# A rarely taken way moved behind the usual one: flag, checks, gathers and row steps in another order

## The chip, the core and the metric

The kernel runs on one core of a Trainium2 chip. A core has a matrix engine (PE), a vector engine (DVE), a scalar engine (ScalarE, ACT in the profile), GpSimd (POOL), SyncE (SP), which here only issues transfers, and 16 DMA engines. Each engine works through its own list of instructions in order; semaphores make one wait for another. The metric is the device time of the whole kernel in microseconds (us).

## The reference

Input are `x` (2708 nodes x 128 features) and a sparse non-negative matrix `adj` (2708 x 2708). Four graph layers follow each other, each `x = layernorm(x + layer(x, adj))`:

```python
# 0: normalised adjacency
h = (d[:, None] * (adj + I) * d[None, :]) @ x;  h @ W.T + b
# 1: attention
XW = x @ W;  s_col = XW @ a[:f];  s_row = XW @ a[f:]
den = exp(leaky_relu(s_row[:, None] + s_col[None, :], 0.01))
num = adj @ den
att = where(num != 0, den / num, 0)
H = adj @ (att @ XW)
# 2: hyperbolic layer: matvec, bias, logmap, adj @ xt, expmap, relu
# 3: (adj > 0) @ x and (adj < 0) @ x times node weights, adj @ x times edge weights, biases by the diagonals
```

Only the piece from the end of layer 0 to layer 1, and the very end, are touched here.

## The kernel before

**Two ways.** Layer 1 as written needs a product of 2708 x 2708 matrices. The kernel avoids it. `den[i, j]` is an exponential of a sum, on either side of a kink, so it splits into a product of a factor for i and one for j on each side. If the nodes are sorted by their scores in 26 groups (`GM`) of at most 126, then for one group most of the numerator is a sum over whole rows of `adj`, carried from group to group, and only the group's own 126 rows need gathering. This holds only if the scores and row sums are in bounds, no element of `adj` is negative and the nodes fit the groups. `good`, `okb`, `below0` and the product `gps` check that and leave `flag_i` (L1313 to L1324): 0 where the fast way may be taken. If it is not, the general way (`dense_attention`, `general_rest`) computes everything after layer 0 densely. With the inputs of the reference the fast way is taken. The flag is read into a register of each engine (L1833); a branch leads to the general way, which stands first, or past it to the fast one.

**Before the flag.** Layer 0 streams `adj` in blocks of 4 x 128 rows by 512 columns. Its end normalises `x`, projects it (`xw`, the scores `rc`; L989 to L1008), stores `xw` to DRAM as `xw_d` (L1009) and counts for each node how many sampled scores lie above it (L1048). Meanwhile SyncE fetches most blocks of `adj` again as `B` (`fill_tile`, L821), for the *row steps*: `whole_sum` (L800), called through `sum_rows`, multiplies the 128 rows of one tile by `e1` and adds them to one row of sums, `tot`. There are 22 steps, nine products each; they are strewn over the sort stage so that PE has work while other engines sort. A block's place is freed when its four steps are done, and the next block fetched into it. At the end ScalarE copies `tot` into `carry0` (L1390), the start of the carried sum.

**Sorting.** DVE finds the borders of the groups: `prev` from the counts (L1206), transposed (L1220), then 26 dependent comparisons with an accumulator, `v` (L1237). Between the row steps PE spreads scores over partitions (`rb`) for `q_b` (L1228). From the borders come one-hot matrices `oh` for the rows' order (i = 0) and the columns' (i = 1), and the packed values `val` (tile number, partition, score in three bf16 `terms`, occupancy; L1278 to L1330). Products with a triangle of ones, `low` (L1293, L1303), count places, giving `slot`; for each of 22 tiles a one-hot `ohs` (L1345) and a product into `list` (L1347) scatter the nodes into 26 x 128 lists. List 0 gives `row_i`, which rows of `adj` to gather; list 1 gives `xw_i`, `gj_l`, `occ_l`, `inval`. `group_matrix` (L707, L708) makes from them the weight matrix of a group; the first three go into `w_first`.

**Groups.** `grouped_attention` takes the columns in two halves of 1354. For each half and group: gather 128 rows by an indirect transfer from POOL (L1427, four buffers), copy the two carried rows into the next group's gather (L1475), multiply (`num`, L1471), take the reciprocal as `exp(-ln)` on ScalarE (L1476, L1483), `att = max(q_b * gj, 1)` (L1465, three buffers) times that (L1484), and aggregate with the group's gathered rows of `xw` into `uacc` (L1436). The rows of `xw` (L1405) are gathered in the first half, one group's after its gather of `adj`. `fast_rest` then does the end of layer 1 and layers 2 and 3 in products with `adj`, streamed in pieces `cb`.

**Order.** A scheduler places the instructions of each engine; `queued(engine)` fixes the order of the marked ones, and `tc.issue_after(x)` places one behind x. Tiles come from pools; memory of a closed pool is used again by a later one, and a tile on it waits for the last users.

## Time and profile before

| | us |
|---|---|
| median of 3 runs | 922.99 (921.04 to 926.29) |
| the profiled execution itself | 920.86 |
| its span, first to last instruction | 919.1 |
| PE busy in it | 855.1 (93%) |
| DVE busy | 556.7 (61%) |
| ScalarE busy | 373.9 (41%) |
| POOL busy | 149.0 (16%) |

The span starts with the first recorded instruction; times in the text count from there. By stages: layer 0 and the sort to about 232, the first half of the groups to about 356, the second to about 494, the rest to 919. In a line of the timeline there stand the start, the length, the engine, the line of the source, the operation, what is written from what, the number of instructions merged, and in brackets how long the engine idled before and what released it. "Issue" means that it waited for nothing that the profile shows: register loads and branches are such. PEld is the loading of weights into PE, which runs beside its products; SPq a transfer's issue on SyncE.

### The profile page before, as it was taken

How to read it: one execution, taken by the hardware profiler on the slowest of the kernel's cores; microseconds unless marked ns; L12 is line 12 of the kernel's file. 1: busy time of each engine (PE TensorE's matmuls, PEld its weight loads, DVE VectorE, ACT ScalarE, POOL GpSimd, SP SyncE). 2: the span in 40 equal slices, each digit the busy share in tenths (PEclk: the TensorE clock that was granted, in tenths of full speed). 3: DMA queues.
4: the chain of work that ended last, by engine and by line, in shares of the span. 5: the costliest groups of instructions: out<-in, count | busy, mean ns of one | idle time of the engine just before them, and what ended most of it. 6: DMA issues, size and time to landing. Idle time of an engine off the chain costs nothing.

```text
span 919.1 us, 9408 instructions
## 1 busy us (share of the span) xinstructions
PE 855.1 (93%) x3268; PEld 428.0 (47%) x3268; DVE 556.7 (61%) x1209; ACT 373.9 (41%) x618; POOL 149.0 (16%) x180
## 2 busy tenths in 40 slices
PE   3799999677899999999999999989999989999997
PEld 3344544334444444444444444454444545555555
DVE  3885558896888888787874114456654464333222
ACT  3786343112777776666662113445322221000000
POOL 5321000411765553222200000000000000000000
PEclk9799999989999999999999999999999989999999
DMA  9996584692794444444323777386864373646410
GB/s 337 361 361 238 71 244 144 218 383 85 242 377 150 156 145 148 134 138 150 124 89 126 249 268 269 125 313 218 321 239 155 128 275 131 238 167 224 152 47 15
DMA packets 95833, 182.83 MB, mean 199 GB/s; under 512 B 6430, under 2 KB 23535, under 8 KB 95652
## 3 DMA queue, kind: packets, MB, share of 16 engines
q1 hardware_dynamic: 85556, 142.37, 44.6%
q0 software_dynamic: 8352, 37.76, 12.6%
q10 hardware_dynamic: 1872, 2.04, 0.7%
q8 instruction: 27, 0.44, 0.2%
q14 instruction: 26, 0.21, 0.1%
HBM read 179.33 MB, written 2.84 MB: 198 GB/s over the span
## 4 chain that ended last, share of the span: by engine, by line
PE 64%; DVE 8%; issue 1%; ACT 1%; ACTq 0%
PE a L1528 22%; PE uacc L1436 14%; PE a L1807 11%; PE num L1471 7%; PE a L1816 6%; DVE att L1484 4%; DVE att L1465 2%; PE pp L1765 1%; PE mx L1635 1%; PE su L252 1%; PE st_l L252 0%; PE gb L707 0%; ACT ln L1476 0%; PE pr_l L274 0%; ACT ln L1483 0%
## 5 line engine op out<-in xcount | busy, mean ns | idle before, releaser
L1436 PE MATMUL uacc<-att,xw_g 128*128 128x512 f32 (+1 forms) x312 | 130.5, 555 | 8.9 <-DVE att L1484 8.2
L1476 ACT ACTIVATE ln<-num,inval,occ_l 128x512 f32<-128x512 f32 (+1 forms) x156 | 106.3, 721 | 66.7 <-DVE gat L1475 64.4
L1807 PE MATMUL a<-cb,ut 128*128 128x512 f32 (+2 forms) x264 | 125.1, 556 | 0.1
L1816 PE MATMUL a<-mask,node 128*128 128x512 f32 (+2 forms) x264 | 120.1, 536 | 1.2 <-DVE mask L1795 1.2
L1471 PE MATMUL num<-gat,w_all 128*128 128x512 f32 (+1 forms) x276 | 114.1, 543 | 0.0
L1528 PE MATMUL a<-cb,q_b 128*128 128x512 f32 (+2 forms) x264 | 111.9, 562 | 1.6 <-DMA cb<-in_adjT_dram 1.6
L1528 PE MATMUL a<-cb,xw 128*128 128x512 f32 (+2 forms) x264 | 107.4, 550 | 0.0
L863 PE MATMUL a<-A,q_b 128*128 128x512 f32 (+2 forms) x264 | 105.8, 549 | 0.0
L1427 POOL DMA_INDIRECT gat<-in_adjT_dram,row_i x52 | 76.6, 1473 | 139.0 <-PE num L1471 77.2
L1436 PEld LDWEIGHTS uacc<-att,xw_g 128*128 128x128 f32 x312 | 55.8, 189 | 90.8 <-issue 50.0
L1475 DVE COPY gat<-num 2x512 f32<-2x512 f32 x150 | 85.9, 608 | 2.9 <-PE num L1471 2.7
L1484 DVE TENSOR_TENSOR att<-att,ln 128x1354 f32<-128x1354 f32 x52 | 81.1, 1559 | 9.5 <-ACT ln L1483 9.5
L1816 PEld LDWEIGHTS a<-mask,node 128*128 128x128 f32 (+1 forms) x264 | 48.1, 191 | 50.3 <-issue 47.9
L1465 DVE TENSOR_SCALAR att<-q_b,gj_l 128x1354 f32<-128x1354 f32 x52 | 47.8, 923 | 37.9 <-PE uacc L1436 36.6
L1471 PEld LDWEIGHTS num<-gat,w_all 128*128 128x128 f32 x276 | 51.3, 191 | 41.3 <-issue 23.4
L1483 ACT ACTIVATE ln<-ln 128x1354 f32<-128x1354 f32 x52 | 69.3, 1333 | 1.3
L1795 DVE TENSOR_SCALAR mask<-cb 128x3072 fp32r<-128x3072 f32 (+5 forms) x24 | 33.5, 1395 | 58.8 <-PE a L1816 58.7
L863 PEld LDWEIGHTS a<-A,q_b 128*128 128x128 f32 (+1 forms) x264 | 46.0, 191 | 48.2 <-issue 47.7
L1528 PEld LDWEIGHTS a<-cb,q_b 128*128 128x128 f32 (+1 forms) x264 | 45.1, 191 | 46.7 <-issue 42.8
L231 ACT ACTIVATE sq_l<-s 128x512 f32<-128x512 f32 (+1 forms) x11 | 6.6, 603 | 147.4 <-DVE s L1825 116.8
L1528 PEld LDWEIGHTS a<-cb,xw 128*128 128x128 f32 (+1 forms) x264 | 45.0, 190 | 46.3 <-issue 46.3
L1071 ACT ACTIVATE xw<-A 128x2048 f32<-128x2048 f32 (+3 forms) x36 | 57.0, 1583 | 8.6 <-DMA b_s<-in_b_dram 4.9
(445 smaller groups left out, 893.8 us busy)
## 6 DMA issues: line engine op xcount, KB each, us to landing
cb<-in_adjT_dram SPq DMA_DIRECT2D x15, 2816.0 KB
cb<-in_adjT_dram SPq DMA_DIRECT2D x15, 2560.0 KB
A<-in_adjT_dram SPq DMA_DIRECT2D x25, 1024.0 KB
B<-in_adjT_dram SPq DMA_DIRECT2D x18, 1024.0 KB
cb<-in_adjT_dram SPq DMA_DIRECT2D x3, 814.0 KB
cb<-in_adjT_dram SPq DMA_DIRECT2D x3, 740.0 KB
ut<-in_adjT_dram SPq DMA_DIRECT2D x2, 1024.0 KB
A<-in_adjT_dram SPq DMA_DIRECT2D x5, 296.0 KB
```

Of the source, the lines that this page charges most:

```text
L863: nc.tensor.matmul(acc[c][:, :w], lhsT=z[:kw, k, :], rhs=t[:kw, i, :w], start=c not in begun, stop=(d == NB - 1 and k == NT - 1), skip_gro ...
L1427: return nc.gpsimd.indirect_dma_start(out=gat[g], out_offset=None, in_=adj_h, in_offset=bass.IndirectOffsetOnAxis(ap=row_i[:, h, g : g + 1 ...
L1436: nc.tensor.matmul(uacc[c][:, : cb - ca], lhsT=xw_g[:, g, :], rhs=att[:, ca:cb], start=(g == 0), stop=(g == GM - 1),)
L1465: nc.vector.tensor_scalar(att, q_b[:, h0 : h0 + HALF], gj_l[:, g : g + 1], 1.0, op0=ALU.mult, op1=ALU.max)
L1471: nc.tensor.matmul(num[:, : cb - ca], lhsT=(w_first if g < FIRST else w_all)[:, g, :], rhs=gat[g][:, ca:cb], start=True, stop=True)
L1475: nc.vector.tensor_copy(gat[g + 1][0:2, ca:cb], num[0:2, : cb - ca])
L1476: nc.scalar.activation(ln_n[:, ca:cb], num[:, : cb - ca], AF.Ln, scale=occ_l[:, g : g + 1], bias=inval[:, g : g + 1],)
L1483: nc.scalar.activation(ln_n, ln_n, AF.Exp, scale=-1.0)
L1484: nc.vector.tensor_mul(att, att, ln_n)
L1528: nc.tensor.matmul(acc[:, :w], lhsT=weights[:kw, k, :], rhs=pc[:kw, t, :w], start=(k == 0), stop=(k == NT - 1),)
L1807: nc.tensor.matmul(acc[:, :w], lhsT=edge[:ke, k, :], rhs=pc[:ke, t, :w], start=(k == 0), stop=False, skip_group_check=True,)
L1816: nc.tensor.matmul(acc[:, :w], lhsT=node[:kw, k, j, :], rhs=mask[:kw, t - ma, :w], start=False, stop=(k == NT - 1 and j == 1), skip_group_ ...
```

## The change

1. The fast way is now straight code after the sort, with no branch before it. At the very end the flag is loaded, and the general way follows under `if flag > 0`. As it would find `x` overwritten, `x` is saved to DRAM (`x_d`) at the start of the groups and read back there.
2. The checks leave the sort stage. `fit_nodes` (POOL) is issued in the second half of the groups at group 6, `checked` (DVE and one product on PE) at group 13.
3. The gathers of the first three groups stand together, their rows of `xw` behind all three.
4. Row steps: 2 instead of 3 before the transposes of `prev`; 3, 3, 1, 1, 1, 1 ahead of the six broadcasts instead of 1 behind each and 3 at the end; 2 before list 0 and one at its tiles 8 and 16, instead of 4 before it; 2 before list 1 as before.
5. The tile number in `val` is made on ScalarE by 22 copies per list with a constant scale, no longer by a product with `tile_b` on POOL; one-hots `ohs` have ten buffers, not four; parts of the sort are held in their written order on DVE and ScalarE; the load of the activation table at the start of the fast way is gone.

```diff
@@ -114,7 +114,6 @@
         return t
 
     iota_b = iota("iota_b", P, 0, 1, 0, BF16)
-    tile_b = iota("tile_b", NT, 0, 1, 0, BF16)
     part_f = iota("part_f", 1, 0, 1, 1)
     node_z = iota("node_z", NT, -N, P, 1)
     unit0 = iota("unit0", 2, 0, -1, 1)
@@ -698,6 +697,7 @@
     xw_i = col.tile([P, GM], I32, tag="xw_i", name="xw_i")
 
     flag_i = col.tile([1, 1], I32, tag="flag_i", name="flag_i")
+    v = col.tile([P, GM + 1], F32, tag="v", name="v")
     sc = col.tile([P, GM], F32, tag="sc", name="sc")
     bi = col.tile([P, GM], F32, tag="bi", name="bi")
 
@@ -725,6 +725,7 @@
 
     xw = const.tile([P, NT, F], F32, tag="xw", name="xw")
     xw_d = tc.dram_tile([NP, F], F32, name="xw_d")
+    x_d = tc.dram_tile([P, NP], F32, name="x_d")
     diag_d = tc.dram_tile([N, 1], F32, name="diag_d")
     w_col = w1ext[:, F : F + 1]
     w_row = w1ext[:, F + 1 : F + 2]
@@ -1214,7 +1215,7 @@
                     )
             nc.vector.tensor_tensor(prev[:, 0, :], prev[:, 0, :], prev[:, 1, :], op=ALU.max)
             prev_ps = ps_tile("prev_ps")
-            sum_rows(3)
+            sum_rows(2)
             with queued(PE):
                 for q in range(len(SAMPLES)):
                     nc.tensor.transpose(
@@ -1222,15 +1223,14 @@
                     )
             for b in range(NB):
                 w, cs = width(b), bslice(b)
+                sum_rows(3 if b < 2 else 1)
                 with queued(PE):
                     pr = bcast_block(rcl[:, 0, :], b, f"rb{b}")
-                    whole_sum(1)
-                nc.scalar.activation(q_b[:, cs], pr[:, :w], AF.Exp, scale=0.99)
-            sum_rows(3)
+                with queued(ACT):
+                    nc.scalar.activation(q_b[:, cs], pr[:, :w], AF.Exp, scale=0.99)
             prev_row = srt([P, NS], "prev_row", F16)
             nc.vector.tensor_copy(prev_row, prev_ps[:, :NS])
 
-            v = srt([P, GM + 1], "v")
             nc.vector.memset(v[:, 0:1], 1.0)
             for g in range(GM):
                 junk = srt([P, NS], f"jk{g}", F16, 2, "jk")
@@ -1253,16 +1253,6 @@
             nc.gpsimd.tensor_sub(terms[:, 2], rest, terms[:, 1])
 
 
-            good = srt([P, NT], "good")
-            fits = srt([P, NT], "fits")
-            nc.gpsimd.tensor_scalar(good, row_sum, 1e-10, None, op0=ALU.is_ge)
-            for val, lo, hi in ((row_sum, 0.0, 1e10), (rc[:, :, 0], -RC_MAX, RC_MAX), (rc[:, :, 1], -RC_MAX, RC_MAX)):
-                for bound, op in ((lo, ALU.is_ge), (hi, ALU.is_le)):
-                    nc.gpsimd.tensor_scalar(fits, val, bound, None, op0=op)
-                    nc.gpsimd.tensor_mul(good, good, fits)
-            nc.gpsimd.tensor_mul(good, good, valid)
-
-
             upto = srt([P, 2, NT], "upto")
             nc.vector.tensor_sub(upto, counted[:, :, :NT], counted[:, :, 1:])
             vs = srt([P, GM + 1], "vs")
@@ -1275,15 +1265,18 @@
             grid = [P, NT, GM]
             t_a = BW // GM
             for i in range(2):
-                nc.vector.tensor_tensor(
-                    c3[i],
-                    vs.unsqueeze(1).to_broadcast([P, NT, GM + 1]),
-                    upto[:, i, :].unsqueeze(2).to_broadcast([P, NT, GM + 1]),
-                    op=ALU.is_le,
-                )
-                nc.vector.tensor_sub(oh[i], c3[i][:, :, :GM], c3[i][:, :, 1:])
-                nc.gpsimd.tensor_mul(val[i][:, :, 0, :], oh[i], tile_b.unsqueeze(2).to_broadcast(grid))
-                nc.scalar.activation(val[i][:, :, 1, :], oh[i], AF.Copy, scale=part_f)
+                with queued(DVE):
+                    nc.vector.tensor_tensor(
+                        c3[i],
+                        vs.unsqueeze(1).to_broadcast([P, NT, GM + 1]),
+                        upto[:, i, :].unsqueeze(2).to_broadcast([P, NT, GM + 1]),
+                        op=ALU.is_le,
+                    )
+                    nc.vector.tensor_sub(oh[i], c3[i][:, :, :GM], c3[i][:, :, 1:])
+                with queued(ACT):
+                    nc.scalar.activation(val[i][:, :, 1, :], oh[i], AF.Copy, scale=part_f)
+                    for t in range(NT):
+                        nc.scalar.activation(val[i][:, t, 0, :], oh[i][:, t, :], AF.Copy, scale=float(t))
             low = {}
             for i in range(2):
                 for h, (ta, tb) in enumerate(((0, t_a), (t_a, NT))):
@@ -1308,21 +1301,6 @@
                                 stop=(t == tb - 2),
                                 skip_group_check=True,
                             )
-            below0 = srt([P, 1], "below0")
-            okb = srt([P, 1], "okb")
-            nc.vector.tensor_reduce(below0, neg_sum, AX.X, ALU.add)
-            nc.vector.tensor_scalar(below0, below0, 0.0, None, op0=ALU.is_le)
-            nc.vector.tensor_scalar(okb, v[:, GM : GM + 1], float(NS), None, op0=ALU.is_equal)
-            nc.vector.tensor_mul(okb, okb, below0)
-            gs = srt([P, 1], "gs")
-            nc.vector.tensor_scalar(good, good, okb, None, op0=ALU.mult)
-            nc.vector.tensor_reduce(gs, good, AX.X, ALU.add)
-            gps = ps_tile("gps")
-            with queued(PE):
-                nc.tensor.matmul(gps[0:1, 0:1], lhsT=gs, rhs=ones[:, 0:1], start=True, stop=True)
-            sum_rows(4)
-            nc.vector.tensor_scalar(flag_i, gps[0:1, 0:1], float(N), None, op0=ALU.not_equal)
-
 
             lists = []
             for i in range(2):
@@ -1338,10 +1316,11 @@
                 nc.vector.tensor_reduce(slot[:, i, :], pos[i], AX.X, ALU.add)
                 nc.vector.tensor_scalar(slot[:, i, :], slot[:, i, :], 2.0, None, op0=ALU.add)
                 ps = ps_tile(f"list{i}")
-                if i:
-                    sum_rows(2)
+                sum_rows(2)
                 for t in range(NT):
-                    ohs = srt([P, P], f"ohs{i}_{t}", BF16, 4, "ohs")
+                    if i == 0 and t in (8, 16):
+                        sum_rows(1)
+                    ohs = srt([P, P], f"ohs{i}_{t}", BF16, 10, "ohs")
                     nc.vector.tensor_scalar(ohs, iota_b, slot[:, i, t : t + 1], None, op0=ALU.is_equal)
                     with queued(PE):
                         nc.tensor.matmul(
@@ -1391,6 +1370,29 @@
 
     marks = {}
 
+
+    good, fits = c_tile("good"), c_tile("fits")
+
+    def fit_nodes():
+        nc.gpsimd.tensor_scalar(good, row_sum, 1e-10, None, op0=ALU.is_ge)
+        for val, lo, hi in ((row_sum, 0.0, 1e10), (rc[:, :, 0], -RC_MAX, RC_MAX), (rc[:, :, 1], -RC_MAX, RC_MAX)):
+            for bound, op in ((lo, ALU.is_ge), (hi, ALU.is_le)):
+                nc.gpsimd.tensor_scalar(fits, val, bound, None, op0=op)
+                nc.gpsimd.tensor_mul(good, good, fits)
+        nc.gpsimd.tensor_mul(good, good, valid)
+
+    def checked():
+        below0, okb, gs = (c_tile(n, 1) for n in ("below0", "okb", "gs"))
+        nc.vector.tensor_reduce(below0, neg_sum, AX.X, ALU.add)
+        nc.vector.tensor_scalar(below0, below0, 0.0, None, op0=ALU.is_le)
+        nc.vector.tensor_scalar(okb, v[:, GM : GM + 1], float(NS), None, op0=ALU.is_equal)
+        nc.vector.tensor_mul(okb, okb, below0)
+        nc.vector.tensor_scalar(good, good, okb, None, op0=ALU.mult)
+        nc.vector.tensor_reduce(gs, good, AX.X, ALU.add)
+        gps = ps_tile("gps")
+        nc.tensor.matmul(gps[0:1, 0:1], lhsT=gs, rhs=ones[:, 0:1], start=True, stop=True)
+        nc.vector.tensor_scalar(flag_i, gps[0:1, 0:1], float(N), None, op0=ALU.not_equal)
+
     def grouped_attention(u_sb):
         adj_h = adjT.rearrange("k (h w) -> (k h) w", h=2)
         chunks = [(0, BW), (BW, 2 * BW), (2 * BW, HALF)]
@@ -1416,6 +1418,7 @@
                 nc.vector.tensor_scalar(u_sb[:kw, t, :], pu[:kw, :P], e2[:kw, t : t + 1], None, op0=ALU.mult)
 
             nc.gpsimd.memset(ut[:, N:], 0.0)
+            nc.sync.dma_start(out=x_d, in_=x)
             for h in range(2):
                 h0 = h * HALF
                 uacc = [acc_tile(c, f"uacc{h}_{c}") for c in range(3)]
@@ -1443,7 +1446,8 @@
 
                 for g in range(3):
                     rows_of = gather(g)
-                    if h == 0:
+                if h == 0:
+                    for g in range(3):
                         with tc.issue_after(rows_of.ins):
                             group_xw(g)
                 carried = nc.vector.tensor_copy(gat[0][0:2, :], carry0[:, h0 : h0 + HALF])
@@ -1457,6 +1461,12 @@
                             group_matrix(w_all, g + 3)
                             with tc.issue_after(rows_of.ins):
                                 group_xw(g + 3)
+                    if h and g == GM // 4:
+                        with tc.issue_after(rows_of.ins):
+                            fit_nodes()
+                    if h and g == GM // 2:
+                        with tc.issue_after(weighted.ins):
+                            checked()
                     if h and g < HALF // P:
                         node_major_u(g)
                     ln_n = mp.tile([P, HALF], F32, tag="ln_n", name=f"ln{h}_{g}", bufs=2)
@@ -1481,7 +1491,7 @@
                             bias=inval[:, g : g + 1],
                         )
                     nc.scalar.activation(ln_n, ln_n, AF.Exp, scale=-1.0)
-                    nc.vector.tensor_mul(att, att, ln_n)
+                    weighted = nc.vector.tensor_mul(att, att, ln_n)
                     if pending is not None:
                         aggregate(*pending)
                     pending = (g, att)
@@ -1497,7 +1507,6 @@
 
 
         rot = {"n": 0}
-        latest.clear()
 
         def scratch(name):
             tag, nb = (("acc3", 1), ("ps", 2), ("acc4", 1), ("ps", 2), ("acc5", 1))[rot["n"] % 5]
@@ -1830,54 +1839,55 @@
+    with tc.tile_pool(name="cb_a", bufs=2) as cb_a:
+        u_sb = xw
+        grouped_attention(u_sb)
...
+            fast_rest(u_sb, pieces, rest_p, blk2)
+
     flag = nc.values_load(flag_i, min_val=0, max_val=1)
-    with tc.If(flag > 0) as cmp:
+    with tc.If(flag > 0):
         with tc.tile_pool(name="any", bufs=1) as any_p, tc.tile_pool(name="blk", bufs=2) as blk:
             pools["big"] = any_p
             pools["blk"] = blk
+            nc.sync.dma_start(out=x, in_=x_d)
             u_sb = big_tile("z2", "u_any")
             dense_attention(u_sb, xw_d, rc, w_row, w_col)
             general_rest(u_sb)
-    with cmp.Else():
-        nc.scalar.preload_act_table_set("natural_log_exp_and_others")
-        with tc.tile_pool(name="cb_a", bufs=2) as cb_a:
-            u_sb = xw
-            grouped_attention(u_sb)
...
-                fast_rest(u_sb, pieces, rest_p, blk2)
```

## The prediction

> **What bounds the kernel now.** I read the page first: TensorE (PE) is busy 93% of the 919.1 us span, so only places where PE waits, or where something bigger than its slack moves, can change the time. The stages by windows show where: 240 to 340 us, the first half of the groups, has PE busy 99.65 of 100 us; 380 to 480, the second half, 94.99; the sorting stage, 170 to 240, is where PE idles. The chain of waits through the handover from sorting to groups (start, length, what):
>
> ```profile
> 226.10 0.23 ACT gj_l L1378
> ...
> 228.07 3.47 issue
> 231.54 0.66 PE gb L707 x2
> 232.20 2.84 PE num L1471 x4
> ```
>
> 228.07 is the flag. Each engine loads it into a register and jumps over the general way; PE does nothing for 3.47 us. The timeline of the same place (start, length, engine, line, operation, idle before it):
>
> ```profile
> 221.34 1.24 POOL L1427 DMA_INDIRECT gat<-in_adjT_dram,row_i  x1 [8.59 <-PE list L1347]
> ...
> 227.51 0.94 POOL L1427 DMA_INDIRECT gat<-in_adjT_dram,row_i  x1 [0.30 <-issue]
> ...
> 229.63 0.19 DVE L1401 COPY w_all<-sc 128x23 f32<-128x23 f32 x1 [3.48 <-issue]
> ...
> 229.89 0.85 DVE L1449 COPY gat<-xw 2x1354 f32<-2x1354 f32 x1
> 230.01 4.05 POOL L1427 DMA_INDIRECT gat<-in_adjT_dram,row_i  x1 [0.30 <-issue]
> ...
> 237.73 1.69 DVE L1475 COPY gat<-num 2x512 f32<-2x512 f32 x3 [1.58 <-PE num L1471]
> ```
>
> Gather 0 is issued at 221.34, gathers 1 and 2 only after the rows of `xw` of the group before them, which need the second list. VectorE (DVE) idles 3.48 us at the jump. Gather 2 arrives late: the copies at 237.73, which write into it, start although their product was ready sooner. The sort stage, again from the timeline:
>
> ```profile
> 197.04 0.40 PEld L800 LDWEIGHTS t<-B,e 128*1 128x1 f32 x12 [0.86 <-DMA B<-in_adjT_dram]
> ...
> 203.95 1.11 DVE L1318 TENSOR_SCALAR good<-good,okb 128x22 f32<-128x22 f32 x1
> ...
> 210.27 2.87 PE L800 MATMUL t<-B,e 128*1 128x512 f32 x37
> ...
> 215.04 3.60 PE L1347 MATMUL list<-val,ohs 128*128 128x156 bf16 x22
> ...
> 226.10 0.23 ACT L1378 ACTIVATE gj_l<-list_s 128x26 f32<-128x26 f32 x1 [1.59 <-DVE list_s L1373]
> ```
>
> PE waits for a `B` block at 197.04. The check product and four row steps hold it from 210.27 until the first list starts at 215.04, and DVE, with four one-hot buffers, waits too. `good` takes 1.11 us for 22 elements: beside it GpSimd (POOL) runs the `tile_b` products (2.98 us for two). `gj_l` at 226.10 closes the lists. Last, transfers (the last two columns are the share of the DMA engines and GB/s):
>
> ```profile
> 168.00:170.00 2.00, 2.00 (x27) 0.98 (x30) 1.85 (x13) 1.11 (x6) 1.75 (x5) 1.00 0.22 67
> 170.00:172.00 2.00, 1.00 (x18) 0.34 (x10) 2.00 (x7) 0.00 (x0) 1.66 (x5) 1.00 0.65 153
> 172.00:174.00 2.00, 0.00 (x0) 0.00 (x0) 1.97 (x12) 0.32 (x2) 1.59 (x5) 1.00 0.88 299
> 174.00:180.00 6.00, 4.25 (x34) 1.71 (x38) 5.86 (x24) 0.00 (x0) 3.74 (x6) 0.72 1.05 396
> 180.00:209.00 29.00, 24.03 (x272) 11.93 (x265) 25.83 (x71) 4.71 (x8) 2.98 (x2) 0.88 1.05 382
> ```
>
> From 174 to 209 the queues are full: nothing can be added there for free.
>
> **What the skill says.** "Runtime: NRT & Kernel Launch", Instruction fetch mechanics: a taken branch to a target outside the prefetched window must fetch its page before going on. The trace agrees: 3.5 us on DVE, 3.9 on PE (227.58 to 231.51), but 0.8 on POOL, which skips a handful of instructions (flag at 211.74, next work 212.56). "SBUF — State Buffer", Who interferes with whom: DVE in a two-port mode and GpSimd lock each other out; the 1.11 us `good` fits. "ScalarE: Activation LUTs", What ACT_TABLE_LOAD costs: an ACTIVATE with immediates is 186 ns + 0.833 ns per element, with 93 ns of overlap; so I estimate 0.12 us for each of the new 26-element copies, and two such here start 0.13 us apart (219.99 and 220.12).
>
> **The change, part by part**, on the clock of this profile.
>
> 1. Two row steps, not three, before the transposes of `prev`. Three took 5.17 us (176.49 to 181.66), a warm one takes 1.28 (182.56 to 183.84): transposes at 180.38. DVE had waited from 180.03, so its 26-step chain ends at 198.62, not 199.90.
>
> 2. `x` is saved to DRAM: 128 x 2816 x 4 B = 1.44 MB. The built order puts it on SyncE's queue behind the fourth `xw` write and ahead of the last two and of fifteen `B` loads. `x` is final at 167.1; bytes move from about 168.9. From there to 174 the queues could move 5.1 us x 385 GB/s = 1.96 MB, and already move 1.04 (last fence). So 0.52 MB, 1.4 us, is pushed into the full stretch; bounds 0 and 3.7 us (nothing hidden). The last `B` of the third block row arrives at 198.4, not 197.04. In the new PE order one broadcast (0.45), a whole row step (1.28) and another broadcast (0.35) follow it: `low` starts at 200.6 against 202.02. Its operand is ready at 200.0.
>
> 3. The checks leave DVE: `okb` 0.15 and 1.09, `good` 1.11, `gs` 0.16, plus their share of the lock; the six `terms` products end near 205.3, not 208.38, and slot 0 near 207.5. The `tile_b` products go to ScalarE as 44 copies, about 5.3 us from 200.7, needed at 210: hidden. `low` took 8.3 us, partly at half clock; PE now warms up earlier, 7.4, until 208.0.
>
> 4. Row steps: two (2.4) before list 0, one at its thirds. 208.0 + 2.4 + 1.1 + 1.2 + 1.1 + 1.2 + 0.8 (22 list products with ten buffers, about 0.135 each between the 0.164 of this trace and 0.11 of the low products) = 215.8. The step at t = 8 needs the last `B` row: 210.3 + 1.4 = 211.7 against a turn at 211.5: just covered. Without cover the 3.7 us case costs 2.3 more. List 0 ended at 218.64. Two row steps, then list 1, whose last twelve one-hots pace it: 215.8 + 2.4 + 2.6 = 220.8 against 224.8. `gj_l` ends 1.56 later as now: 222.4 against 226.33.
>
> 5. Three gathers first. I expected them early; the waits of the built program say no. Gather 0 now waits for the last product of list 1 and for `gj_l` on ScalarE: its buffer lies over the sorting pool. So it issues at 222.5, later than the 221.34 of now. From issue to the copy that may follow took 4.86 us (221.34 to about 226.2, when its bytes stop): 227.4; copy 0.85; first `num` product at 228.4 against 232.0. Gathers 1 and 2 follow it 1.25 us apart and arrive by about 231.9, before the copies that want them, so the 0.9 us that gather 2 costs today at the first `att` goes too. Together **-4.4 us** when the aggregation starts. The jump's 3.5 us is inside this, it doesn't come on top; the table load (1.28 us, ScalarE not waited for) adds nothing.
>
> 6. First half of the groups: same work, another order. In it the multiply of a group stands more often behind the release of `att` by the aggregation before it; PE has 2.57 us of work between those two (products of 0.86, 0.55 and 0.86, a transpose of 0.3), the chain needs 2.45. Bounds 0 and 1.5 (0.1 on some 15 groups); I take **+0.3**.
>
> 7. The checks in the second half. Fourteen POOL instructions, which take 7.1 us today (167.35 to 174.44), stand between gathers 9 and 10 of this half; a gather is issued every 5.04 us and is three groups ahead, so this takes 2.1 us of some 15. Behind them only gathers. On DVE seven small instructions and the flag. The period there is a chain:
>
> ```profile
> 431.86 0.93 DVE L1465 TENSOR_SCALAR att<-q_b,gj_l 128x1354 f32<-128x1354 f32 x1 [1.04 <-PE uacc L1436]
> ...
> 432.70 1.56 DVE L1484 TENSOR_TENSOR att<-att,ln 128x1354 f32<-128x1354 f32 x1
> ...
> 434.32 2.54 PE L1436 MATMUL uacc<-att,xw_g 128*128 128x512 f32 x6 [0.23 <-DVE att L1484]
> ```
>
> Aggregation, release, `att` multiply, aggregation: 5.04 us, PE idle for only 0.25. In the built order DVE stops at the flag until PE has done two of the three aggregation chunks and the check product; behind it wait the copy of the next group, `att`, two more copies, and the multiply that PE waits for. Multiply to multiply start was 5.04; here 2.54 + 0.86 (a product moved ahead) + 0.15 + 0.59 + 0.25 + 1.2 (two copies) + 1.57 = 7.16: +2.1. The next two multiplies stand ahead of their releases and can win back up to 0.5 us a group, what PE has free. **+1.0**; bounds 0 and 2.2.
>
> 8. The flag at the end. Today DVE's last work ends at 916.47, the last output is issued at 916.50 and the span ends 2.6 us later. Now DVE loads the flag and jumps over the general code: 3.5 us, so about 0.9 past today's end, and SyncE must jump as well after issuing: **+1.2**; bounds 0 (hidden by the write) and 2.7 (PE's 3.9 on the last engine).
>
> Sum: -4.4 + 0.3 + 1.0 + 1.2 = **-1.9 us** on the profiled execution's own 920.86 (span 919.1 and 1.8 around it), so 919.0; that run was 2.1 under the median of 922.99, and the same step from the median gives **921.1**.
>
> **Rivals.**
> - *The handover wins all of it.* The `x` write hides (another 1.4), the checks and the order cost nothing, the jump hides behind the last write: -5.8, **917.2**, and with gathers landing earlier than I think, 916. For it: PE has slack behind the check, and DMA idles at 168. Against: gather 0's new wait, and DVE's jump with only 2.6 us of cover.
> - *The check unhinges the second half.* If the order after it does not regain its lead, each of the 12 groups left pays another 0.55 us (one 2x330 copy before the multiply): 6.6, with the 2.2 of the stall: -4.4 + 0.3 + 2.2 + 1.2 + 6.6 = +5.9, **928.9**: slower. It decides once a group there takes over 5.4 us. Against: PE's order falls back to the old pattern within five groups.
> - *The flag only moves.* What the middle loses, the end pays: the whole 3.9 us beyond today's last work plus a full `x` write (2.3 uncovered): -4.4 + 2.3 + 0.3 + 1.0 + 2.7 = +1.9, **924.9**; no change, by the bound below.
> - *The early gathers do issue early* (the wait I read is met sooner): at 219, first `num` near 225.5: -7.4, and with the other terms -4.9, **918.1**.
>
> **How the numbers follow.** A measurement of this kernel tells about 0.5%, 4.6 us, from no change. My sum 0.46; all won 0.26; flag only moves 0.12; early gathers 0.08; unhinged 0.08. Terms uncertain by 1.5 (lists and gathers), 1.4 (`x`), 1 (check), 1 (end) reach some 3 us either side of the sum, and the rivals stretch it: 915.5 to 925.5 leaves out about 2 in 10. Faster than 918.4: the two winning rivals and a little of the sum, 0.39; slower 0.09; same 0.52.
>
> **What would show it.** Right: no idle of 3 us between the last `gb` and the next product; gather 0 issued just after `gj_l`, near 222.5; first `num` near 228.5; list 0 ending near 216; one group near 7 us in the second half, neighbours at 5.0; engines idle 3 us after their last work. Wrong: gather 0 issued before list 1; `B` waits reaching into list 0 by over 2 us; a first-half group over 5.0 us; the end no longer than 2.6 us after the last output.

## The result and the profile after

The changed kernel is slower: 931.07 us median of 13 runs (926.74 to 934.68) against 923.24 of 13 before (921.04 to 926.29), ratio 1.0075 with a 95% interval from 1.0057 to 1.0092. The forecast was 921.1, range 915.5 to 925.5. The profiled execution took 928.29 us, its span is 926.5, against 919.1 before: +7.4, in line with the medians (+7.8).

To see where the time goes I marked the same events in both profiles. "C" is the first comparison of VectorE that counts scores (`counts`, in layer 0), which both kernels reach by the same instructions in the same order; the later events are given from C, by their starts where nothing else is said.

| event | before | after | difference of the step |
|---|---|---|---|
| C, from the span's start | 134.75 | 136.07 | +1.3 |
| `gj_l` done, from C | 91.58 | 87.29 | (-4.3) |
| gather 0 issued | 86.59 | 88.20 | (+1.6) |
| first `num` product | 97.25 | 94.58 | (-2.7) |
| first aggregation | 106.22 | 103.91 | -2.3 |
| multiply of group 20, first half | 200.58 | 199.10 | +0.8 |
| multiply of group 25, first half | 222.93 | 225.28 | +3.8 |
| from there to group 25 of the second half | 132.18 | 133.98 | +1.8 |
| from there to the last VectorE work | 426.61 | 425.70 | -0.9 |
| from there to the end of the span | 2.63 | 5.45 | +2.8 |

A number in brackets compares the times from C themselves. The others compare the step from the last line without brackets, and add up to the +7.4 but for rounding. So the lists of the sort stage ended as early as forecast, and 2.3 of that was left at the first aggregation. Then the first half gave back 4.6, where 0.3 was forecast, the second half 1.8, and the end 2.8.

In the sort stage `low` starts no earlier than before (67.48 from C, before 67.27), but it is done in 5.95 us and not 8.30. The lines of before and then of the changed kernel:

```profile
202.02 0.57 PE L1293 MATMUL low<-val,upper 128*128 128x494 bf16 x1 [4.25 <-DVE val L1284]
202.39 3.91 PE L1303 MATMUL low<-val,ones_b 128*128 128x468 bf16 x18
...
203.55 0.38 PE L1286 MATMUL low<-val,upper 128*128 128x494 bf16 x1
203.78 2.07 PE L1296 MATMUL low<-val,ones_b 128*128 128x468 bf16 x18
```

Before, PE had idled 4.25 us and the granted clock over `low` was 0.70 of full speed; now row steps and broadcasts stand right ahead of it, there is no idle, and the clock is 1.00.

The handover. The chain of waits in the changed kernel (start, length, what):

```profile
223.13 0.23 ACT gj_l L1357
...
223.41 0.70 PE gb L707 x2
...
224.27 5.38 DMA gat<-in_adjT_dram,row_i
...
229.74 0.86 DVE gat L1453
...
230.65 4.85 PE num L1481 x8
```

The idle 3.47 of "issue" is gone, and in its place stands a transfer: gather 0 goes out only at 224.27, 0.91 behind `gj_l`, and everybody waits 5.4 us for it. Then the end of the first half, in the timeline of the changed kernel (start, length, engine, line, operation, idle before it):

```profile
341.01 2.19 POOL L1430 DMA_INDIRECT gat<-in_adjT_dram,row_i  x1 [2.21 <-PE num L1481]
...
347.24 0.85 DVE L1453 COPY gat<-xw 2x1354 f32<-2x1354 f32 x1 [3.26 <-DMA gat<-in_adjT_dram,row_i]
348.02 1.55 DVE L1494 TENSOR_TENSOR att<-att,ln 128x1354 f32<-128x1354 f32 x1
...
349.63 4.22 PE L1439 MATMUL uacc<-att,xw_g 128*128 128x512 f32 x6 [2.39 <-DVE att L1494]
```

and in that of the kernel before:

```profile
346.54 2.54 PE L1436 MATMUL uacc<-att,xw_g 128*128 128x512 f32 x6 [0.23 <-DVE att L1484]
...
348.00 0.84 DVE L1449 COPY gat<-xw 2x1354 f32<-2x1354 f32 x1
```

The copy `gat<-xw` starts the carried sum of the *second* half: it writes the row sums into that half's first gather. Before, VectorE took it when the gather had landed, with no idle. Now it stands one multiply earlier in VectorE's list, ahead of that of group 22. It waits 3.26 us for the gather issued at 341.01, the multiply behind it waits too, and PE waits 2.39 for the multiply. Then six products take 4.22 us in place of 2.54: PE came back at half clock (granted 0.60 over these 4.22 us, 1.00 over the six products before). Group 22 takes 7.19 us and group 24, the next behind the slow products, 7.23, where 5.0 to 5.7 are usual.

The flag in the second half, timeline of the changed kernel:

```profile
431.37 1.56 DVE L1494 TENSOR_TENSOR att<-att,ln 128x1354 f32<-128x1354 f32 x1
...
435.12 0.15 DVE L1394 TENSOR_SCALAR flag_i<-gps 1x1 int32<-1x1 f32 x1 [0.83 <-PE gps L1393]
436.18 0.68 DVE L1485 COPY gat<-num 2x512 f32<-2x512 f32 x1 [0.91 <-PE num L1481]
...
439.07 1.57 DVE L1494 TENSOR_TENSOR att<-att,ln 128x1354 f32<-128x1354 f32 x1
```

Multiply to multiply is 7.70 here, 5.04 otherwise: +2.66. The next two take 4.03 and 4.02 and win back 2.03, and the two after them 5.57 and 5.66 and lose 1.15 again. The end, first of the kernel before and then of the changed one:

```profile
916.16 0.31 DVE L290 TENSOR_TENSOR ob<-s,rs 128x148 f32<-128x148 f32 x1
916.50 0.37 SPq L1831 DMA_DIRECT2D out_dram<-ob  x1
...
920.72 0.31 DVE L289 TENSOR_TENSOR ob<-s,rs 128x148 f32<-128x148 f32 x1
921.06 0.37 SPq L1840 DMA_DIRECT2D out_dram<-ob  x1
```

The span ends at 926.5, 5.45 us behind VectorE's last work; before it was 2.63. Last the transfers, by windows (columns as in the prediction):

```profile
170.00:172.00 2.00, 2.00 (x35) 0.85 (x28) 2.00 (x9) 0.46 (x3) 0.00 (x0) 1.00 1.01 406
180.00:209.00 29.00, 26.78 (x304) 12.44 (x296) 26.21 (x75) 8.23 (x41) 0.00 (x0) 0.90 1.05 384
```

The write of `x` fills the stretch from 170 that was two thirds full. PE now waits for `B` until 199.58 (197.04 before), and once more inside list 0 until 213.93.

### The profile page after: what moved, and what is told of

Read it like the earlier page. It is cut to its first block, busy times and chain, and to the rows that moved or that the text cites. A ratio compares the mean times of both kernels' runs of the same rounds, so it can differ in the third digit from the quotient of the medians.

```text
span 926.5 us, 9413 instructions
## 1 busy us (share of the span) xinstructions
PE 856.0 (92%) x3268; PEld 426.7 (46%) x3268; DVE 556.0 (60%) x1209; ACT 377.3 (41%) x661; POOL 147.4 (16%) x176
## 4 chain that ended last, share of the span: by engine, by line
PE 75%; DMA 10%; DVE 10%; ACT 2%; issue 2%; POOL 0%; SPq 0%; DVEq 0%; ACTq 0%; POOLq 0%
PE a L1537 21%; PE uacc L1439 12%; PE a L1816 11%; PE a L864 9%; PE num L1481 7%; PE a L1825 6%; DVE att L1494 4%; DMA A<-in_adjT_dram 4%; DMA B<-in_adjT_dram 3%; DMA cb<-in_adjT_dram 2%; DVE att L1475 2%; PE t L801 1%; DMA gat<-in_adjT_dram,row_i 1%; PE pp L1774 1%; DVE counts L1049 1%
## 5 line engine op out<-in xcount | busy, mean ns | idle before, releaser
L1439 PE MATMUL uacc<-att,xw_g 128*128 128x512 f32 (+1 forms) x312 | 132.4, 561 | 13.0 <-DVE att L1494 12.0
L1430 POOL DMA_INDIRECT gat<-in_adjT_dram,row_i x52 | 80.3, 1544 | 169.6 <-PE gb L707 74.7
```

The source lines that it names most:

```text
L1430: return nc.gpsimd.indirect_dma_start(out=gat[g], out_offset=None, in_=adj_h, in_offset=bass.IndirectOffsetOnAxis(ap=row_i[:, h, g : g + 1 ...
L1439: nc.tensor.matmul(uacc[c][:, : cb - ca], lhsT=xw_g[:, g, :], rhs=att[:, ca:cb], start=(g == 0), stop=(g == GM - 1),)
```

## The experiments

Each run is the changed kernel with one edit, if nothing else is said. The kernel before ran beside each of them (medians 923.1 to 923.8), and ratios are to that. The ratio of the changed kernel was 1.0075; an interval of a run is some 0.2%, 2 us, to either side. A single part of 1 to 4 us is therefore seen in its place in the profile, and the timed runs alone would hardly tell it from nothing.

**The copy for the second half, placed later.**

```diff
-                carried = nc.vector.tensor_copy(gat[0][0:2, :], carry0[:, h0 : h0 + HALF])
+                with tc.issue_after(muls[GM - 3].ins) if h else nullcontext():
+                    carried = nc.vector.tensor_copy(gat[0][0:2, :], carry0[:, h0 : h0 + HALF])
```

> The changed kernel, but VectorE takes the copy that starts the carried sum of the second half only after the multiply of group 23, eight instructions later than in the built order of the changed kernel. Theory (that copy stands too early on VectorE and holds back the multiply of group 22 until the second half's first gather lands, 3.3 us; PE idles 2.4 us and then runs six products in 4.2 us rather than 2.5): groups 22 to 25 of the first half take 5.0 to 5.7 us each, the second half starts 3.5 to 4 us earlier, and the time falls from 931.1 to about 927.3. Rival (the gather is late for everybody, and the next taker of it waits instead): the stall turns up at the first product of the second half and the time stays within 1 us of 931.1.

Measured: 929.02, ratio 1.0063 (1.0042 to 1.0084). Groups 22 to 24 take 5.02, 5.04 and 5.03 instead of 7.19, 4.02 and 7.23, and group 25 comes 3.45 us earlier from C (221.83 against 225.28). In its timeline the copy waits for nothing and PE is fed:

```profile
346.17 1.56 DVE L1497 TENSOR_TENSOR att<-att,ln 128x1354 f32<-128x1354 f32 x1
...
347.79 2.54 PE L1440 MATMUL uacc<-att,xw_g 128*128 128x512 f32 x6 [0.23 <-DVE att L1497]
...
353.10 0.84 DVE L1455 COPY gat<-xw 2x1354 f32<-2x1354 f32 x1
```

The theory holds in the profile: 3.45 of the 3.8 come back. The median fell by 2.0, with an interval that overlaps that of the changed kernel; what shows clearly in timed runs is this edit together with three others, at the end of this section.

**No flag at the end.** The load of the flag, the jump and the general way are left out.

> The changed kernel without its last part: the flag is computed but not loaded, and neither the jump nor the general way is there. Theory (the jump over the general way costs what lies between the 2.6 us that followed the last output before and the 5.5 us after): the span ends 2.6 us after the last VectorE instruction, and the time falls by 2.9 us to about 928.2. Rival (the longer end is the last transfer's, or noise of one profile): the end stays above 4.5 us and the time within 1 us of 931.1.

Measured: 929.40, ratio 1.0066 (1.0044 to 1.0089); the span ends 3.00 behind VectorE's last work, 2.4 less. The median fell by 1.7 only. This kernel's second half is 0.9 longer (134.88): the groups behind 13 stand in another order than in the changed kernel and win nothing back.

**The jump at the end, over short code.**

```diff
             nc.sync.dma_start(out=x, in_=x_d)
-            u_sb = big_tile("z2", "u_any")
-            dense_attention(u_sb, xw_d, rc, w_row, w_col)
-            general_rest(u_sb)
```

> The changed kernel with the load of the flag and the jump at its end, but the general way behind it is cut down to one transfer. Theory (the price of the jump lies in its distance: each engine must fetch the instructions behind the general way): the span ends about 3 us after the last VectorE instruction, as without any flag (3.0), and the time falls by 2 to 2.5 us to about 928.8. Rival (loading the flag on every engine and meeting again behind the branch cost it): the end stays at 5 us or more and the time within 0.7 us of 931.1.

Measured: 928.31, ratio 1.0049 (1.0034 to 1.0063). The flag is loaded and the jump is taken, and the end is 2.97, as without any flag. So of the 5.45 some 2.5 is the distance of the jump; loading the flag and branching cost nothing that shows. This agrees with what the prediction took from the Trainium skill ("Runtime: NRT & Kernel Launch", Instruction fetch mechanics): a taken branch must fetch when its target lies beyond what was prefetched.

**Early gathers.** The first two write into `ut`, which lay idle and shares no memory with the sort.

```diff
-                    gat[g] = mp.tile([P, HALF], F32, tag="gat", name=f"gat{h}_{g}", bufs=4)
+                    if h == 0 and g < 2:
+                        gat[g] = ut[:, g * HALF : (g + 1) * HALF]
+                    else:
+                        gat[g] = mp.tile([P, HALF], F32, tag="gat", name=f"gat{h}_{g}", bufs=4)
```

> The changed kernel, but the first two gathers of the first half write into the two halves of the tile ut, which is idle until the end of that half and never lay under the sorting stage; nothing else is changed. Theory (the only thing that held gather 0 back to 224.27 was the memory it shares with the sorting stage): gather 0 is issued at about 219, 1 us after its indices, and has landed by 225; the first product follows the first weight matrix at about 225.5 to 226.5 instead of 230.65, and the time falls by 4 to 5 us, to about 926.5. Rival (the indices, GpSimd's queue or the later gathers set the start): gather 0 moves, but the second and third product or the first aggregation wait for gather 2 or the rows of xw, and less than 1.5 us is left: 929.6 or more.

Measured: 928.92, ratio 1.0060 (1.0039 to 1.0082). Gather 0 is issued at 82.55 from C instead of 88.20, the first product at 91.37 instead of 94.58. The wait was the memory, as the theory says; the third gather, still on the old memory, waits 5.8 us for `gj_l`. The gain is 3.2 and not 4 to 5, since a new wait appears on VectorE:

```profile
222.04 0.32 DVE L1335 COPY list_s<-list 128x156 f32<-128x156 f32 x1 [0.34 <-PE list L1326]
223.87 0.85 DVE L1456 COPY ut<-xw 2x1354 f32<-2x1354 f32 x1 [1.50 <-DMA ut<-in_adjT_dram,row_i]
224.65 0.17 DVE L1337 SCALAR_TENSOR_TENSOR list_s<-list_s 128x26 f32<-128x26 f32 x1
```

The copy that starts the *first* half's carried sum was now planned ahead of the small operations of list 1, and holds them, and so `gj_l`, by 1.5 plus 0.85: the same fault as at group 22. Group 22 still takes 7.22 here.

**The tests behind the groups, left to the scheduler.** Only `checked()` moves, behind `node_major_u`.

> The changed kernel, but the last piece of the tests (seven small VectorE instructions, one product, the flag) stands behind the groups and not at group 13 of the second half; GpSimd's part stays where it is. Theory (VectorE stops at the flag there, and the order around it makes the multiply of group 13 late by 2.7 us, of which some 1.8 are never regained): the second half keeps its 5.0 us a group throughout and the time falls by 1.8 us to about 929.3. Rival (the loss is GpSimd's, whose fourteen instructions delay a gather, or the order after it): the long group stays and the time with it, within 0.7 us of 931.1.

Measured: 933.90, ratio 1.0122 (1.0097 to 1.0147): worse. Group 13 takes 5.04, but group 5 now 8.14:

```profile
398.88 0.23 POOL L1382 TENSOR_TENSOR good<-good,valid 128x22 f32<-128x22 f32 x1
399.14 0.24 DVE L1390 TENSOR_SCALAR good<-good,okb 128x22 f32<-128x22 f32 x1 [4.13 <-POOL good L1382]
```

With no order of its own, the piece that needs GpSimd's result was planned in group 5, and VectorE stood there for 4.13 us until GpSimd had it ready. The run doesn't tell the two theories apart; it was repeated with an order.

**The tests behind the groups, kept there.**

```diff
-                    if h and g == GM // 2:
-                        with tc.issue_after(weighted.ins):
-                            checked()
...
+            with tc.issue_after(weighted.ins):
+                checked()
```

> The changed kernel, but the VectorE and TensorE part of the tests stands behind the last multiply of the groups, kept there by an order, so that VectorE waits neither for the flag nor for GpSimd's part inside a group. Theory (the flag inside group 13 costs what the multiplies of the second half lose from there on, 2.7 us less 2.0 regained plus 1.1 lost again): every group from 5 to 23 of the second half takes 5.0 to 5.7 us, and the time falls by 1 to 2 us from 931.1, to about 929.5. Rival (GpSimd's fourteen instructions hold a gather back): one group between 6 and 12 grows by 2 us and the time stays at 931 or more.

Measured: 928.94, ratio 1.0067 (1.0051 to 1.0083). The second half takes 132.18, to a hundredth what it took before, so the flag's place costs the 1.80 and GpSimd's part of the tests nothing.

**No write of `x`.**

> The changed kernel without the write of x to memory (nor the reading back of it in the general way, which is left incomplete). The order of all other instructions is the same. Theory (the write pushes the fetches of B by 1.4 to 2.2 us, and the row steps before and inside list 0 wait for them): counted from the start of counting, the waits for B fall to below 0.5 us in all, list 0 ends 1 to 1.5 us earlier, and the time falls by about 1 us to 930. Rival (TensorE's own work and the one-hot matrices pace both lists, the waits are covered): the end of list 1, counted the same way, moves by less than 0.4 us.

Measured: 930.49, ratio 1.0079 (1.0063 to 1.0095), not apart from the changed kernel. In the profile `gj_l` is done at 86.15 from C, 1.1 earlier, and the first product at 93.14, 1.4 earlier; the waits of PE for `B` fall from 2.2 to 1.7, not below 0.5. The theory is right in its direction, and the waits that remain were not the write's.

**The first gathers as before**, each followed by its rows of `xw`.

> The changed kernel with the first gathers as before: after each of the first three gathers of adj the rows of xw of its group. Theory (TensorE and ScalarE, at half clock and in turn, pace the first three groups, and gather 2 is not waited for in either order): the first aggregation starts within 0.4 us of where it does in the changed kernel, counted from the first product, and the time stays within 0.7 us of 931.1. Rival (as in the prediction, gathers in front save 0.9 us at group 2): the copies into gather 2 wait for it, and the time rises by about 0.9.

Measured: 932.18, ratio 1.0098 (1.0078 to 1.0117). Here the rival is nearer: the copy into gather 2 waits 0.98 for it, and from first product to first aggregation it takes 11.17. The changed kernel takes 9.33 (9.80 in a second profile), and two variants with the same order there took 10.86 and 10.82. These four differ by PE's clock: it stood at half for the first 2.9, 3.9, 6.0 and 5.9 us behind the first product, and half of that difference is what the times differ by. In this run it stood at half for 3.0 us, which would make about 9.4; so the old order costs 1.8 here, twice the prediction's 0.9. The edit also changed the order of VectorE's `att` instructions at this place, so the 1.8 is not shown to be the gathers' alone.

**The row steps and four one-hot buffers as before.**

```diff
-            sum_rows(2)
+            sum_rows(3)
...
-                sum_rows(3 if b < 2 else 1)
...
+                    whole_sum(1)
+            sum_rows(3)
...
+            sum_rows(4)
...
-                sum_rows(2)
+                if i:
+                    sum_rows(2)
...
-                    if i == 0 and t in (8, 16):
-                        sum_rows(1)
-                    ohs = srt([P, P], f"ohs{i}_{t}", BF16, 10, "ohs")
+                    ohs = srt([P, P], f"ohs{i}_{t}", BF16, 4, "ohs")
```

> The changed kernel with the row steps where they were before (three ahead of the transposes of prev, one after each spread of the scores, three behind, four ahead of list 0) and four one-hot buffers instead of ten; tests and copies stay as changed. Theory (of the 4.3 us by which the lists end earlier, counted from the counts, some 3 come from this order and the rest from the tests that left VectorE): the lists end 2.5 to 3.5 us later, gather 0 with them, and the time rises to about 934. Rival (the lists end early only because the tests left): they move by less than 1 us.

Measured: 932.06, ratio 1.0091 (1.0073 to 1.0109). In its profile `gj_l` is done at 91.48 from C, where it was before the change (91.58): all of the 4.3 comes from the order of the row steps and the buffers, and with the old order the tests that left VectorE bring nothing that shows. Half of it arises at `low`: here PE idles 3.63 us ahead of it again and it takes 7.48. The same holds throughout. The seven profiles with the old order have 2.7 to 4.9 us of idle ahead of `low`, a clock of 0.67 to 0.82 over it and 7.2 to 8.6 us for it; the eleven with the new order have no idle, 0.95 to 1.00, and 5.9 to 6.2 us. The median rose by only 1.0, though, less than the profile's 4.2; why the timed runs show so little of it stays open.

**One part alone: only the general way moved.** The kernel before, with the fast way first, the general one under the flag at the end, and `x` saved. As in the changed kernel, the load of the activation table is gone, and so is one place where the fixed orders start afresh.

> The kernel before with one part of the change alone: the general way stands behind the usual one under the flag at the end, and x is saved to memory for it. Tests, sorting stage and the order of the first gathers are those of before. Theory (taking the branch out of the middle lets the scheduler plan sort and groups as one piece, and that piece has three new waits: gather 0 behind the weights of the groups and TensorE's last list product, the copy for the second half ahead of the multiply of group 22, the jump at the end): gather 0 is issued about 0.9 us behind gj_l and the first product starts 1 to 2 us later than before, not earlier; a group of 7.2 us at 22; the end 5.5 us instead of 2.6; together 8 to 10 us, 932 to 934. Rival (the flag only moves: 3.5 us saved at the handover, 2.5 to 2.9 paid at the end, the groups as before): 922 to 924.

Measured: 934.22, ratio 1.0121 (1.0093 to 1.0149). This settles where the loss is from. The sort is as before (`gj_l` at 91.48 from C), yet gather 0 is issued at 92.40 instead of 86.59, in its timeline:

```profile
231.34 1.24 POOL L1429 DMA_INDIRECT gat<-in_adjT_dram,row_i  x1 [20.96 <-PE gb L707]
...
236.67 0.85 DVE L1451 COPY gat<-xw 2x1354 f32<-2x1354 f32 x1 [5.89 <-DMA gat<-in_adjT_dram,row_i]
```

The first product comes 1.4 us later than before (98.64), though no engine jumps any more; group 22 takes 7.29, and the end 5.34. All of it comes with the branch; the write of `x`, tried alone below, is at most 1.8 of the 10.8 us. The waits of the built programs say why gather 0 moved: before, its buffer waited for the last row step and for `row_i`; with the ways in the other order it waits for the last product of list 1 and for `gj_l`, since the pools fall on other memory. For the changed kernel the early gathers have shown this; for this kernel it is the same 0.9 us behind `gj_l` that speaks for it. And sort and groups are now one piece of code with no branch between: the scheduler plans them together, and the order of the groups on VectorE in this kernel is nearly that of the changed one. The changed kernel as a whole is some 3 us faster than this one: its other parts win back that much of what the branch loses.

**The write of `x` alone, in the kernel before.** All other engines keep their order.

> The kernel before with the write of x to memory added, at the same place in SyncE's queue as in the changed kernel, and read back only in the general way; every other engine keeps its order. Theory (the write pushes the fetches of B, as removing it from the changed kernel gave 1.6 us at the end of list 1): the wait for B at 197.04 grows, and the one hidden at list 0 may show; the time rises by 1 to 2 us. Rival (before, the row steps come later against the fetches and cover it): less than 0.7 us. If the write or its 1.44 MB of memory also sets layer 0's start, counting starts later than 135.5.

Measured: 924.19 (14 runs), 923.06 before, ratio 1.0008 (0.9997 to 1.0019). In the profile the rival is right: the last `B` comes 1.2 us later from C (63.49, before 62.30), yet the first product comes at 96.77, no later than before, so in the old order the sort stage covers the write. The times don't decide between the two, since the interval reaches from -0.3 to +1.8 us. The 1.6 that the expectation quotes for the changed kernel is 1.1 at the end of list 1. And its last sentence came true: counting started at 139.46.

**Layer 0: chance or change?** Three more profiles without an edit.

> The kernel before, unchanged, a third profile. Of eleven profiles of the changed kernel, its variants and the kernel before with the branch at its end, counting starts at 134.8 to 138.9 us (mean 136.6); in both profiles of the kernel before at 134.7. Theory (chance of the single execution, from the arrival of the first blocks of adj): this one and the next lie in 134.7 to 138, at least one of the two above 135.5. Rival (something in the change, its instructions in memory or the place of its tiles, slows layer 0 by some 2 us): both again at 134.5 to 135.2.

> The kernel before, a fourth profile, for the same question: by the theory of chance counting starts somewhere in 134.7 to 138 us, by the rival again at 134.5 to 135.2.

> The changed kernel, a second profile. Theory (chance) and rival (the change slows layer 0): counting starts at 134.7 to 138 by the theory, at 136 or later by the rival. The stall of the copy for the second half (group 22 at 7.2 us), the long group 13 and the end of 5.5 us turn up again in either case, since the orders are fixed.

Measured, with an earlier one announced thus:

> The kernel before, unchanged, profiled a second time. In layer 0 both kernels have the same instructions in the same order on the engines that set its pace, yet the five profiles of the changed kernel and its variants start counting (the first product of VectorE with the samples) at 135.8 to 138.0 us, the one profile of the kernel before at 134.75. Theory (arrival of the first blocks of adj varies from one execution to the next): this profile lies somewhere between 134.5 and 138. Rival (the change slows layer 0, by its place in memory): again 134.5 to 135.

C lies at 134.75, 134.70, 136.32 and 136.10 in four profiles of the kernel before, at 136.07 and 136.85 in two of the changed one, and between 134.79 and 139.46 in the twelve other profiles. Two of four above 135.5 is what chance was to show, and the ranges overlap; the means (135.5, and 136.8 over the fourteen with parts of the change) still differ by 1.3. In all 18 profiles the last 81.5 us before C are the same, so the difference arises in the first 53 to 58 us; there PE waits for blocks of `adj`, for some 10 us in every profile and in most once more, near 42 us, for up to 2.4. The two latest starts, 138.94 and 139.46, are the two variants of the kernel before that write `x`; the changed kernel without the write, at 134.84, fits with the write as a cause, but one with it started at 134.79. So some of the 1.3 may belong to the change, by a way that no run here shows. The second profile of the changed kernel repeats the rest: group 22 at 7.21, group 13 at 7.71, the end at 5.45.

**All together.** The two copies, the early gathers and the tests, mended as above:

```diff
+                with tc.issue_after(muls[GM - 3].ins if h else marks["listed"]):
+                    carried = nc.vector.tensor_copy(gat[0][0:2, :], carry0[:, h0 : h0 + HALF])
```

(`marks["listed"]` is the last small operation of list 1; with it the edits of the early gathers and of the tests.)

> The changed kernel with what the runs so far point to: the copy for the second half behind the multiply of group 23, gathers 0 and 1 in ut, the copy that starts the carried sum of the first half behind the last small instruction of list 1 (with the early gathers alone it stood ahead of them and held them back 1.8 us), and the last piece of the tests behind the groups. Theory (the waits are separate, so what each gave adds up: 3.4, 3.2, some 1.5 and 1.8 by the profiles, of which the medians of single runs confirmed about two thirds): 931.1 less 7 to 10, 921 to 924, level with the kernel before or up to 0.25% faster. Rival (they hide each other, since a group that comes earlier waits elsewhere): 926 or more.

Measured: 922.03 (18 runs), 923.46 before, ratio 0.9990 (0.9978 to 1.0001): level with the kernel before, or a little faster, and 9 us faster than the changed kernel. In its timeline gather 0 lands while list 1 is still worked on:

```profile
219.19 1.24 POOL L1433 DMA_INDIRECT ut<-in_adjT_dram,row_i  x1 [39.80 <-DVE samples L1366]
...
225.09 0.92 DVE L1457 COPY ut<-xw 2x1354 f32<-2x1354 f32 x1 [1.62 <-DMA ut<-in_adjT_dram,row_i]
...
226.07 2.08 PE L1483 MATMUL num<-ut,samples 128*128 128x512 f32 x2 [1.04 <-DVE ut L1457]
```

The first product is at 89.42 from C, 7.8 earlier than before; the first half ends at 217.72 (222.93), the second takes 132.20. What it wins there, 5.2, it pays back at the end (5.54 against 2.63) and, in this profile, by a later C. These edits together bring 9 us, clear of the noise, so timed runs too show that the time was lost at these places; the early gathers also give what the kernel before did not have.

## Why the prediction was wrong

The sum was -1.9 and the profile moved by +7.4. Of the 9.3 between them, step 6 is 4.3, step 5 is 2.1, step 8 is 1.6, layer 0 is 1.3 and step 7 is 0.8; the layers behind the groups took 0.9 off. By the prediction's own steps, with the times from C where layer 0's 1.3 would hide them:

- **1 to 4, the sort stage: right in the sum, by luck in its parts.** List 0 was to end at 215.8 and ended at 216.79, `gj_l` at 222.4 and was done at 223.36; without layer 0's 1.3 that is -0.3 for both. The gain of `gj_l`, 3.9 forecast, is 4.3. But two errors cancel: on the same clock the transposes came at 181.3, not 180.4, and `low` started at 202.2, as late as before, not at 200.6; then it took 5.95 us, not 7.4, because PE was warm from its first product on, and ended at 208.2 against 208.0. The last `B`, 198.3 against 198.4, was right. Step 3, the tests off VectorE, gives nothing by itself. Step 2 put the write of `x` at 1.4; taking it out gave 1.1 to 1.4.
- **5, the handover: right in its mechanism, half in its size.** Gather 0 behind `gj_l` was read from the built program and came so, but 0.9 behind it, not 0.1; it took 5.5 to the copy, not 4.9. So the first product gained 2.7, not 3.6. And at the first aggregation 2.3, not 4.4: PE was busy for 9.1 of the 9.3 us in between, before for 8.3 of 9.0, for the same products. Of that some 0.3 is its clock, which the sum left out: 0.50 in the first 2 us and 0.77 in the next, against 0.50 and 0.93. What the rest is stays open. "Three gathers first" is worth up to 1.8 inside the changed kernel, where 0.9 was forecast, but none of it shows against the kernel before: the step from first product to first aggregation grew, from 8.97 to 9.33.
- **6, the order of the first half: the step that failed.** It asked only where the multiplies stand against the releases of `att`, and took +0.3. Up to group 20 that is right within its bounds (0.8). But the new order also moved the copy for the second half ahead of group 22, and the step never asked which *other* instruction of VectorE had changed places, and what it waits for. It costs 3.8 us between groups 20 and 25, more than any other term, beyond the step's upper bound of 1.5; placing the copy later gave 3.45 of it back. Some 1.6 of it is PE's half clock behind the gap: in the two profiles that have the stall but kept the clock, the stretch grew by 2.2, and group 24 took 5.5. That the copy moved at all comes with the branch: it does so in the kernel in which only the branch was moved. The rival that ended on the slow side sat in the second half and missed it too.
- **7, the flag in group 13: under-sized.** 2.66 at the multiply against 2.1; 2.03 is regained, as thought, but then 1.15 lost again. 1.8 against +1.0, inside its bounds. GpSimd's part costs nothing where it stands, as said; what it costs when VectorE must wait for it was seen, 4.13 us.
- **8, the end: under-sized.** It let the jump of 3.5 run beside the 2.6 of the last write and took 1.2. The end grew by 2.8, over its upper bound of 2.7: the jump's 2.5 (far against near) comes whole on top, and the other 0.3 is there without a flag too (3.00 against 2.63).
- **Layer 0** was not in the sum, as both kernels have the same instructions there. It adds 1.3 in these two profiles; chance may explain it, and the runs don't exclude that some of it is the change.

Without the one unseen place the profile would stand at about +4 (7.4 less 3.45), and the run with the copy placed later, 929.02, still lies outside the range up to 925.5: the other terms were too kind as well. By number the nearest rival was the unhinged second half, 928.9, but not by its mechanism: the groups behind 13 came back to 5.0 within five groups. In its mechanism "the flag only moves", +1.9 with 0.12, came nearest, and its picture was still too kind: moved alone, with the saving of `x` that it needs, the branch cost 10.8 us. Two of the signs named told nothing, since the profile before shows such groups too: first-half groups over 5.0 us (5.66 and 5.76) and second-half groups over 5.4 (5.66 and 5.88).

## What to carry to other kernels

A branch in the middle of a kernel is also a wall in the plan: here, with it gone, the scheduler ordered the groups anew, and the buffer of the first gather came to wait for later work. Before pricing such a change, go through the order of *each* engine for instructions that changed places, and ask of every one that waits for a transfer what stands behind it. A short copy ahead of a multiply that PE needs is worth an explicit order. Filler work for PE is best placed right ahead of a chain that PE paces: here that kept the clock whole over `low` and saved 2 us. And moving a jump over much code to the very end doesn't hide it: it cost 3.5 us in the middle and still 2.5 at the end.

## What the runs showed of the hardware

- **A gap of 2.3 to 2.7 us can cost PE its clock, or not.** In eleven profiles the copy stands ahead of group 22 and PE idles 2.29 to 2.69 us there. In nine of them the granted clock is half for 3.4 us behind the gap, and the six products take 3.5 to 4.2 us. In the other two (early gathers, gap 2.41; branch moved alone, 2.49) it stays whole and they take 2.54. So the length of the gap alone doesn't decide. The Trainium skill, "TensorE: Matmul & The Clock Gate", What's actually happening, puts the half clock behind at least one idle window of some 3.4 us, and says that this window runs freely; here shorter gaps were enough in most profiles.
- **The clock behind an idle stretch sets how long the next products take.** At the handover it stood at half for 2.9 us behind the first product in the changed kernel and for 6.0 us in a variant with the same order of products; the first aggregation came 9.33 and 10.86 us behind that product. Ahead of `low`, 2.7 to 4.9 us of idle went with 7.2 to 8.6 us for it, no idle with 5.9 to 6.2.
- **A far jump costs 2.5 us more than a near one**: with a whole general way behind the branch the kernel ended 5.3 to 5.8 us behind VectorE's last work, with one transfer in its place 2.97, without any jump 3.00.
